# Cross-attention with image prompts: the last 64 channels' keys in two array halves, the second batch's context transposed by VectorE, the prompts projected in four 32-column tiles

## The chip, the cores and the metric

The kernel runs on one core of a Trainium2 chip. A core has five engines with a queue of instructions each: TensorE (PE, matrix products; its weight loads are listed as PEld), VectorE (DVE), ScalarE (ACT), GpSimd (POOL) and SyncE (SP, which issues most DMA transfers). Data lie in SBUF on 128 partitions; TensorE writes to PSUM banks. Engines wait for each other by semaphores, and each works through its own queue in order. The metric is the device time of one execution in microseconds (us).

TensorE is an array of 128 x 128 cells. A matmul loads weights (contraction on the array's rows, output channels on its columns) and streams a second operand through them. A matmul with fewer output channels uses a strip of the array's columns, one with a shorter contraction a strip of its rows; several strips can hold different weights.

## The reference

Eight batches, 112 queries and 375 context rows each, all float32. The first 371 context rows are text, the last 4 are image prompts. 20 heads of 16 channels, 320 channels in all.

```python
q = heads(x @ W_q); k_t = heads(text @ W_k); v_t = heads(text @ W_v)
probs_t = softmax(q @ k_t^T * scale)
text_out = probs_t @ v_t
k_ip = heads(prompts @ W_k_ip); v_ip = heads(prompts @ W_v_ip)
qsem = l2norm(probs_t @ text)                  # per head and query, 512 wide
sem = qsem @ l2norm(prompts)^T
probs_ip = softmax(q @ k_ip^T * scale + 0.5 * sem) * mask
out = (text_out + probs_ip @ v_ip) @ W_out + b_out + x
```

## The kernel before

The norm of `probs_t @ text` is never formed from the 512-wide rows. The kernel makes the inner products of all context rows with each other once a batch (`gram`, L463, and `first_gram` for batch 0), doubles what lies off the diagonal, and multiplies each head's unnormalised probabilities with these, with the values and with the prompts in one product (`product`, recorded at L710): a 112-row product per head and per block of 32 context rows. Heads are worked in five groups of four; the four heads of a group stand on four strips of 32 array rows. A step is a batch and a group, (b, g).

Per batch there are these stages, written as generators that are advanced piece by piece:

- context: loaded by SP (`load_ctx`, L135) and turned so that embedding lies on partitions (`transposed_context`, L394). Batches 0 and 1 are loaded in whole rows of 2 KB and transposed by TensorE against an identity (L414), with ScalarE and VectorE copying from PSUM (L424, L422). Batches from 2 on are loaded in pieces of 512 bytes and transposed by VectorE alone (L402). The constant `LEAD` = 2 separates them. Behind the text columns come four columns of the normalised prompts (`prompts_behind`, by GpSimd).
- values (`values`, L535): three chunks of 128 context rows, four matmuls each.
- keys (`keys`, L493): three pieces. The first two are 128 channels each, four matmuls over 371 columns. The third holds the last 64 channels, spread with zeros to 128 (each head's 16 channels take a strip of 32), since a head's scores are taken on a strip of 32 rows. For batch 0 (L512) and the last batch (`last_keys`, L526) it is a product like the others, with `wk_sb` spread by GpSimd (`spread`, L124). For batches 1 to 6 these 64 channels are computed along with the values, as 64 further output columns (L543, 384 in place of 320), copied by GpSimd into `k3` (L552) with zeros between, and transposed by TensorE (L503).
- queries (`project_queries`, L319), two batches at a time from batch 1 on: channels on partitions, multiplied by a mask that keeps the even or the odd heads of each strip of 32 (L353). For the last 64 channels only one such copy is made.
- scores (L662), maximum (VectorE, L675), exponential (ScalarE, L679), a DMA that lays the probabilities out anew (`xg`, L686, SP), a VectorE transposition (`xgT`, L698), and the products (L710).
- per group, VectorE multiplies the product with the probabilities and sums (`reduced`, L763), ScalarE takes the value sums (L737). `finish` ends a batch.
- prompts (`prompt_projections`, L275): keys and values of all 32 prompts, as two tiles of 32 array columns and 320 channels each, four matmuls a tile; then transposes and copies.

The order on TensorE, VectorE and SP is written out by hand, and after the opening that of ScalarE and GpSimd too. The opening (from L1020) runs context 0, inner products 0, values 0, queries and keys of the first two groups' heads, the scores of steps (0, 0) and (0, 1), between them the transposes of batch 1's context, then the last pieces of the keys and the first of three pieces of batch 1's inner products. From there the loop runs `alone(0)`, then pairs of steps (`pair`, L1115), and behind each pair `behind` (L1183) slips in the stages of this and the next batch. `behind(0)` holds the other two pieces of inner products, `prompt_projections`, and the first chunk of batch 1's values.

PSUM has eight banks in three rings, `qd` (4), `sc` (2) and `mm` (2). `bank` (L91) takes the next bank of a ring, from the list `turn` if that holds anything; a bank that comes round again has to be free first. The products of step (0, 0) take the four `qd` banks.

## Time and profile before

| | us |
|---|---|
| median of 3 runs | 419.94 |
| lowest and highest | 419.73, 420.93 |
| the profiled execution's own time | 421.54 |
| its span, first to last instruction | 419.8 |
| TensorE busy in the span | 411.7 (98%) |
| VectorE | 322.2 (77%) |
| ScalarE | 185.5 (44%) |
| GpSimd | 116.0 (28%) |

TensorE's granted clock is 0.999 of the full one over the span. Profile lines give an engine, a source line, what is written `<-` what is read, shapes as partitions x elements, and the count `x`. The chain is followed back from the last instruction, at each step to what released it; its pieces add up to the span. A fp32 matmul is listed as two passes, each with its weight load.

### The profile page before, as it was taken

To read this page: it belongs to the slowest core of one execution; us is meant where nothing else is said; L and a number is where in the kernel's file an instruction comes from. 1 tells how busy PE (TensorE), PEld (TensorE's weight loads), DVE (VectorE), ACT (ScalarE), POOL (GpSimd) and SP (SyncE) were. 2 spreads that over 40 slices of the span, in tenths; PEclk is the share of its full clock that TensorE was granted. 3 is DMA by queue.
4 is the path that set the end of the run, shared out by engine and by line. 5 is a ranking of instruction groups with operands and counts; after the bars stand their busy time and mean duration, and the time that the engine had idled before them with its cause. 6 is when DMAs were issued, how large, how long until landed. Compare 5 with 4: busy or idle time off the path is not lost.

```text
span 419.8 us, 13826 instructions
## 1 busy us (share of the span) xinstructions
PE 411.7 (98%) x5511; PEld 314.1 (75%) x5511; DVE 322.2 (77%) x684; ACT 185.5 (44%) x634; POOL 116.0 (28%) x278
## 2 busy tenths in 40 slices
PE   8999999999999999999999999999999999999995
PEld 8866686877677786868686877778776888776893
DVE  4054777897887876886888897887788897789964
ACT  3253333334543642514553464333643464246772
POOL 4302310031161352012051225102124126005570
PEclk9999999999999999999999999999999999999999
DMA  8678966778554656577645575575656345575311
GB/s 249 163 190 246 220 157 165 180 187 181 133 156 125 169 127 170 143 162 160 174 116 138 148 173 144 156 186 138 164 150 168 92 118 149 156 177 169 98 34 29
DMA packets 58002, 64.64 MB, mean 154 GB/s; under 512 B 19016, under 2 KB 51760, under 8 KB 57938
## 3 DMA queue, kind: packets, MB, share of 16 engines
q1 hardware_dynamic: 57054, 62.32, 58.5%
q8 instruction: 44, 0.72, 0.7%
q10 hardware_dynamic: 692, 0.89, 0.7%
q0 software_dynamic: 192, 0.55, 0.6%
q14 instruction: 20, 0.16, 0.1%
HBM read 19.04 MB, written 5.22 MB: 58 GB/s over the span
## 4 chain that ended last, share of the span: by engine, by line
PE 87%; DVE 4%; DMA 3%; ACT 2%; SPq 2%; issue 1%; ACTq 0%; POOL 0%; DVEq 0%; POOLq 0%
PE ps_qd L710 39%; PE ps_v L543 15%; PE ps_k L512 10%; PE ps_g L474 8%; PE ps_s L662 5%; PE ps_q L344 3%; PE ps_o L867 2%; DMA xg<-p 1%; DVE xgT L698 1%; PE ps_g L444 1%; DMA vr<-vd 1%; ACT p L679 1%; PE ps_c L414 1%; DVE nmx L675 1%; SPq L488 1%; DMA ct<-in_ctx_dram 1%
## 5 line engine op out<-in xcount | busy, mean ns | idle before, releaser
L710 PE MATMUL ps_qd<-u,xgT 32*112 32x40 f32 (+11 forms) x3840 | 215.7, 351 | 0.4 <-DVE xgT L698 0.4
L710 PEld LDWEIGHTS ps_qd<-u,xgT 32*112 32x112 f32 x3840 | 177.4, 172 | 38.4 <-issue 7.1
L698 DVE STREAM_TRANSPOSE xgT<-xg 128x768 f32<-128x768 f32 (+1 forms) x63 | 123.1, 1976 | 7.1 <-DMA xg<-p 7.1
L679 ACT ACTIVATE p<-ps_s,nmx 112x371 f32<-112x371 f32 x160 | 85.6, 584 | 58.3 <-DVE nmx L675 57.2
L675 DVE TENSOR_REDUCE nmx<-ps_s 112x1 f32<-112x371 f32 x160 | 77.1, 534 | 36.7 <-PE ps_s L662 34.0
L763 DVE CUSTOM_DVE_ANT_0 p<-ps_qd,p 112x371 f32<-112x371 f32 x150 | 72.7, 544 | 15.9 <-ACT pvs L737 10.4
L629 POOL COPY u<-vr 128x64 f32<-128x64 f32 x120 | 26.7, 236 | 185.0 <-PE ps_qd L710 108.0
L543 PE MATMUL ps_v<-wv_sb,ctxT 128*128 128x384 f32 (+1 forms) x192 | 63.8, 479 | 0.3 <-ACT kT L519 0.3
L662 PE MATMUL ps_s<-kT,qm 32*112 32x375 f32 (+1 forms) x320 | 60.8, 486 | 0.0
L543 PEld LDWEIGHTS ps_v<-wv_sb,ctxT 128*128 128x128 f32 x192 | 35.3, 190 | 21.2 <-ACT kT L519 1.2
L512 PE MATMUL ps_k<-ctxT,wk_sb 128*128 128x371 f32 x136 | 45.8, 481 | 0.0
L737 ACT COPY pvs<-ps_qd 112x21 f32<-112x21 f32 x150 | 21.7, 198 | 52.4 <-DVE ss L763 50.1
L512 PEld LDWEIGHTS ps_k<-ctxT,wk_sb 128*128 128x128 f32 x136 | 24.6, 190 | 13.4 <-ACT ctxT L424 0.5
L474 PE MATMUL ps_g<-ctxT 128*32 128x119 f32 (+11 forms) x672 | 33.3, 344 | 0.6 <-POOL ctxT L390 0.6
L474 PEld LDWEIGHTS ps_g<-ctxT 128*32 128x32 f32 x672 | 25.9, 109 | 8.1 <-issue 4.1
L662 PEld LDWEIGHTS ps_s<-kT,qm 32*112 32x112 f32 x320 | 27.1, 171 | 5.0 <-issue 0.5
L550 ACT COPY vext<-ps_v 128x384 f32<-128x384 f32 (+1 forms) x24 | 11.2, 465 | 37.1 <-PE ps_v L543 37.0
L681 ACT COPY ipl<-ps_s 112x4 f32<-112x4 f32 x140 | 24.0, 172 | 0.0
L353 DVE TENSOR_SCALAR qm<-ps_q,emask 128x224 f32<-128x224 f32 (+1 forms) x25 | 9.0, 398 | 18.5 <-PE ps_q L344 18.5
L460 ACT ACTIVATE ug<-ps_g 128x375 f32<-128x375 f32 (+2 forms) x24 | 9.0, 377 | 29.2 <-DMA ct<-in_ctx_dram 8.4
L519 ACT COPY kT<-ps_k 128x371 f32<-128x371 f32 x17 | 8.0, 469 | 30.5 <-PE ps_k L512 30.5
L402 DVE STREAM_TRANSPOSE ctxT<-ct 128x512 f32<-128x512 f32 x18 | 19.3, 1077 | 0.0
(157 smaller groups left out, 311.6 us busy)
## 6 DMA issues: line engine op xcount, KB each, us to landing
xg<-p SPq DMA_DIRECT2D x158, 162.3 KB
u<-ug SPq DMA_DIRECT2D x128, 99.0 KB
ct<-in_ctx_dram SPq DMA_DIRECT2D x24, 176.0 KB
vip<-vipd SPq DMA_DIRECT2D x7, 560.0 KB
vr<-vd SPq DMA_DIRECT2D x20, 120.0 KB
vd<-vext SPq DMA_DIRECT2D x14, 160.0 KB
vd<-vext SPq DMA_DIRECT2D x28, 40.0 KB
ct<-in_ctx_dram SPq DMA_DIRECT2D x4, 256.0 KB
```

Of the source, the lines that this page charges most:

```text
L474: nc.tensor.matmul(ps[p * RG : (p + 1) * RG, s0 : T - t0], ctxT[:, e, t0 + q * RG : t0 + (q + 1) * RG], ctxT[:, e, t0 + s0 : T], start=(e ...
L512: nc.tensor.matmul(ps[:, :TT], wk_sb[:, e, i * P : (i + 1) * P], s["ctxT"][:, e, :TT], start=(e == 0), stop=(e == NE - 1),)
L543: nc.tensor.matmul(ps[:, :w], ctxT[:, e, c * P : (c + 1) * P], wv_sb[:, e, :w], start=(e == 0), stop=(e == NE - 1),)
L629: nc.gpsimd.tensor_copy(region(b, c)[:, :, UV - c * P :], s["vr"][:, c * QN : (c + 1) * QN, g, :])
L662: nc.tensor.matmul(ps[:S, :w], qm[a * RG : (a + 1) * RG, i, r, j * S : (j + 1) * S], s["kT"][a * RG : (a + 1) * RG, i, :w], start=True, st ...
L675: nc.vector.tensor_reduce(nmx, ps[:S, :TT], AX.X, ALU.max, negate=True)
L679: nc.scalar.activation(p, ps[:S, :TT], AF.Exp, bias=nmx)
L681: nc.scalar.copy(s["ipl"][:, groups[g][a], :], ps[:S, TT:T])
L698: nc.vector.transpose(xT[:, j : j + n].rearrange("p j (k q) -> p q j k", q=QN), xg[:, :, j * RG : (j + n) * RG].rearrange("p q (j k) -> p ...
L710: nc.tensor.matmul(banks[a][:S, j * RG : UW], xT[a * RG : (a + 1) * RG, j, :S], region(b, c)[a * RG : (a + 1) * RG, p, q * RG :], start=(j ...
L737: nc.scalar.copy(s["pvs"][:, h, :], ps[:S, TT:UW])
L763: nc.vector.tensor_tensor_reduce(out=p, in0=ps[:S, :TT], in1=p, scale=1.0, scalar=0.0, op0=ALU.mult, op1=ALU.add, accum_out=s["ss"][:, h : ...
```

## The change

Seven edits, which belong together:

1. The last 64 channels' keys of every batch are made by `last_keys`: for each of the four embedding chunks two matmuls with the same 64 weight columns, the first half of the text rows (186) into PSUM partitions 0 to 63, the second half (185) into 64 to 127. Four ScalarE copies then lay each half into the key tile twice, on partitions 0 to 63 and 64 to 127. The values are 320 columns wide for all batches; `k3`, its copies and transposes and `spread` are gone.
2. A strip of 32 rows in the last key tile now holds two heads. Queries of the last channels get both masked copies (one more VectorE instruction in each of the five query projections), and `scores` chooses strip and copy accordingly. GpSimd copies the last 64 columns of `wq_sb` behind themselves, one instruction instead of four.
3. Batch 1's context is loaded in pieces of 512 bytes (eight transfers in place of four) and transposed by VectorE, called right behind the inner products of batch 0. Its cleared block comes first in GpSimd's queue, and the prompt copy for it stands ahead of the clearing of `xT`.
4. Batch 1's inner products are all three made in the opening, in banks `mm`, `mm`, `sc`.
5. `behind(0)` therefore begins with the prompt projections, in a `qd` bank.
6. The prompts are projected in four tiles of 32 array columns: keys and values, 160 channels each. Three ScalarE copies, one GpSimd copy, and two transfers to DRAM instead of one.
7. `prompt_logits` reads the last heads contiguously.

```diff
-    wk_sb = const.tile([P, NE, CP], F32, tag="wk_sb", name="wk_sb")
-    wv_sb = const.tile([P, NE, C + REST], F32, tag="wv_sb", name="wv_sb")
+    wk_sb = const.tile([P, NE, C], F32, tag="wk_sb", name="wk_sb")
+    wv_sb = const.tile([P, NE, C], F32, tag="wv_sb", name="wv_sb")
...
     def load_ctx(b):
-        if b >= LEAD:
+        if b > 0:
...
     def prompt_projections():
         for e in range(NE):
             for i, w in enumerate((wkip_sb, wvip_sb)):
-                nc.tensor.matmul(
-                    ps[i * N : (i + 1) * N, :C],
-                    ipT[:, e, :],
-                    w[:, e, :],
+                for n, part in enumerate(parts):
+                    m = 2 * i + n
+                    nc.tensor.matmul(
+                        ps[m * N : (m + 1) * N, : C // 2],
+                        ipT[:, e, :],
+                        w[:, e, part],
...
     def project_queries(bs):
-            for r in range(2 if i < FULL else 1):
+            for r in range(2):
...
     def transposed_context(b):
-        if b >= LEAD:
+        if b > 0:
...
     def keys(b):
-        for i in range(NC):
-            ps = bank(f"ps_k_{b}_{i}", spare=0 < b < B - 1 and i == FULL)
-            if 0 < b < B - 1 and i == FULL:
-                for c in range(NT):
-                    nc.tensor.transpose(...)
-                nc.scalar.copy(s["kT"][:, i, :TT], ps[:, :TT])
-                yield
-                return
+        for i in range(FULL):
+            ps = bank(f"ps_k_{b}_{i}")
...
+        last_keys(b, bank(f"ps_k_{b}_{FULL}", spare=0 < b < B - 1))
+        yield
     def last_keys(b, ps):
         for e in range(NE):
-            nc.tensor.matmul(
-                ps[:, :TT], wk_sb[:, e, FULL * P :], s["ctxT"][:, e, :TT], ...
-        nc.scalar.copy(s["kT"][:, FULL, :TT], ps[:, :TT])
+            for n in range(2):
+                nc.tensor.matmul(
+                    ps[n * REST : (n + 1) * REST, : min((n + 1) * KH, TT) - n * KH],
+                    wk_sb[:, e, FULL * P :],
+                    s["ctxT"][:, e, n * KH : min((n + 1) * KH, TT)],
+                    start=(e == 0),
+                    stop=(e == NE - 1),
+                )
+        for n in range(2):
+            t = slice(n * KH, min((n + 1) * KH, TT))
+            for m in range(2):
+                nc.scalar.copy(
+                    s["kT"][m * REST : (m + 1) * REST, FULL, t],
+                    ps[n * REST : (n + 1) * REST, : t.stop - t.start],
+                )
...
     def values(b):
-        w = C + REST if 0 < b < B - 1 else C
-                    ps[:, :w], ctxT[:, e, c * P : (c + 1) * P], wv_sb[:, e, :w],
+                    ps[:, :C], ctxT[:, e, c * P : (c + 1) * P], wv_sb[:, e, :],
...
     def scores(b, g, a, early=False, ps=None):
+        rg = a
+        if i == FULL:
+            rg, r = a // 2 + 2 * (a % 2), a % 2
-            qm[a * RG : (a + 1) * RG, i, r, j * S : (j + 1) * S],
-            s["kT"][a * RG : (a + 1) * RG, i, :w],
+            qm[rg * RG : (rg + 1) * RG, i, r, j * S : (j + 1) * S],
+            s["kT"][rg * RG : (rg + 1) * RG, i, :w],
...
     drain(products)
+    drain(transposed_context(1))
     gram_to_groups(0, range(QN - 1))
...
-    spread(nc.gpsimd, wq_sb)
-    nc.gpsimd.tensor_copy(wv_sb[:, :, C:], wk_sb[:, :, FULL * P : C])
-    spread(nc.gpsimd, wk_sb)
+    nc.gpsimd.tensor_copy(wq_sb[:, :, C:], wq_sb[:, :, FULL * P : C])
...
-    turn[:] = ["mm", "qd", "qd"]
-    drain(transposed_context(1))
-    prompts_behind(1)
     for a in range(GROUP):
         scores(0, 1, a, early=True)
...
-    run(("g", 1), lambda: gram(1))
+    turn[:] = ["mm", "mm", "sc"]
+    run(("g", 1), lambda: gram(1), NT)
...
     def behind(n):
-                turn[:] = ["sc", "mm", "qd", "mm"]
+                turn[:] = ["qd", "mm"]
...
             tr(0)
-            gr(nb, 2)
             if n:
+                gr(nb, 2)
                 f(b - 1)
             else:
                 run(("pp",), prompt_projections)
```

More of the change, by code (lines that the diff above doesn't have):

```diff
@@ L52 @@
     HN = H * NIP
+    KH = (TT + 1) // 2
     VW = NIP + 1 + D
@@ L245, in order_values @@
         )
+    parts = [slice(n * C // 2, (n + 1) * C // 2) for n in range(2)]
     def normalised_prompts():
@@ L310, in prompt_projections @@
         yield
-        nc.sync.dma_start(vipd, kv[N:])
+        for n, part in enumerate(parts):
+            m = 2 + n
+            nc.sync.dma_start(vipd[:, part], kv[m * N : (m + 1) * N, : C // 2])
         yield
@@ L549, in values @@
                 )
[L550 to L555 removed]
+            nc.scalar.copy(vext[:, c, :], ps[:, :C])
             yield
@@ L956, in ending @@
             )
-        parts = [slice(i * C // 2, (i + 1) * C // 2) for i in range(2)]
         ps_o = [bank(f"ps_o_{b}_0", spare=True)]
```

58 lines of the change are left out of this document (14 added, 44 removed).

## The prediction

> **What bounds the kernel now.** I read the page's busy shares and its summary of the chain first, then the chain itself in order of time, the opening 50 us instruction by instruction, the groups by shape, and the busy time in short stretches.
>
> ```profile
> PE 411.7 (98%) x5511; PEld 314.1 (75%) x5511; DVE 322.2 (77%) x684; ACT 185.5 (44%) x634; POOL 116.0 (28%) x278
> PE 87%; DVE 4%; DMA 3%; ACT 2%; SPq 2%; issue 1%; ACTq 0%; POOL 0%; DVEq 0%; POOLq 0%
> ```
>
> TensorE (PE) is busy 98% of the span and carries 87% of the chain, so what it must stream decides almost everywhere; another engine matters only where PE has to wait for it. The chain gives each PE stage its start, its length and its number of passes (one fp32 matmul is two passes, so four matmuls show as x8):
>
> ```profile
> 26.07 1.43 PE ps_c L414 x12
> 27.50 1.21 PE ps_s L662 x6
> 28.70 5.18 PE ps_k L512 x16
> 33.89 2.64 PE ps_g L474 x27
> 36.53 1.15 PE ps_qd L710 x10
> ...
> 41.88 2.19 PE ps_g L474 x43
> 44.07 2.21 PE ps_kv L280 x16
> 46.28 2.78 PE ps_v L543 x8
> 49.05 1.15 PE ps_qd L710 x10
> ...
> 59.91 2.69 PE ps_k L512 x8
> ...
> 101.51 0.32 PE ps_k L503 x3
> 101.83 2.51 PE ps_k L512 x8
> 104.34 5.16 PE ps_v L543 x16
> ...
> 138.09 0.47 PE ps_k L503 x3
> ...
> 359.44 2.17 PE ps_v L543 x8
> ```
>
> The reader should see three prices here. Eight passes over 371 columns take 2.51 us, 0.314 a pass or 0.85 ns a column. The same eight passes take 2.69 (at 59.91) when the stage before used the array in strips: a change of how the array is divided costs 0.18. And ps_kv pushes sixteen passes of 320 columns, alternating between two 32-column strips of the array, through in 2.21 us, the time that eight such passes take in one full-width array (2.17 at 359.44): two strips ran side by side almost perfectly.
>
> **The change, part by part.**
>
> *Last 64 channels, batches 1 to 6.* Gone: 64 of the 384 columns of every value chunk. A chunk goes from 2.58 (half of 5.16, at 104.34) to 2.17, so 0.41 less. There are 18 chunks; the first of batch 1 lies in the opening and is treated there, so 17 x 0.41 = 7.0 us. Gone too: three transposes a batch, 0.32 in odd batches, 0.47 in even ones (which come straight after strip work, so 0.15 of it is the change of division): 3 x 0.32 + 3 x 0.47 = 2.4 us. Added: eight matmuls a batch, 64 output channels each, over 186 or 185 columns, alternating between the two halves of the array's columns. That is sixteen passes at 186 x 0.85 = 0.157: 2.51 us if one after another, 1.26 if in pairs. No row shows 64-column strips; the nearest, ps_kv, shows pairs, so I take 1.26 and keep 2.51 as the other end. 6 x 1.26 = 7.5 us. Changes of division: in even batches the keys stand between products and inner products, one change of 0.18 to get in (the one to the inner products was there); in odd batches between queries and the next keys, two new ones: 3 x 0.18 + 3 x 0.36 = 1.6 us. Sum: -7.0 - 2.4 + 7.5 + 1.6 = **-0.3 us**. So this large-looking part is nearly a wash.
>
> *The opening* needs these rows:
>
> ```profile
> 8.15 0.29 SPq L158 DMA_DIRECT2D ct<-in_ctx_dram  x1
> 14.53 7.77 SPq L488 DMA_DIRECT2D u<-ug  x12
> 14.56 0.28 POOL L327 MEMSET xT<- 64x224 f32 x1
> 20.30 0.82 PE L344 MATMUL ps_q<-xT,wq_sb 128*128 128x112 f32 x6
> 21.16 0.58 DVE L353 TENSOR_SCALAR qm<-ps_q,emask 128x112 f32<-128x112 f32 x2 [11.40 <-PE ps_q L344]
> 25.82 1.95 ACT L679 ACTIVATE p<-ps_s,nmx 112x371 f32<-112x371 f32 x4 [0.52 <-DVE nmx L675]
> 37.03 0.50 SPq L122 DMA_DIRECT2D wip<-in_L_xattn_W_v_ip_dram  x1
> 42.11 0.54 DVE L763 CUSTOM_DVE_ANT_0 p<-ps_qd,p 112x371 f32<-112x371 f32 x1 [2.11 <-ACT pvs L737]
> 43.97 4.50 DVE L698 STREAM_TRANSPOSE xgT<-xg 128x1536 f32<-128x1536 f32 x2
> ```
> ```profile
> L698 DVE STREAM_TRANSPOSE xgT<-xg 128x1536 f32<-128x1536 f32 x17 | 51.5, 3027 | 0.0
> L402 DVE STREAM_TRANSPOSE ctxT<-ct 128x512 f32<-128x512 f32 x18 | 19.3, 1077 | 0.0
> L280 PEld LDWEIGHTS ps_kv<-wip,ipT 128*32 128x32 f32 x16 | 1.2, 110 | 0.7
> ```
> ```profile
> 13.00:14.00 1.00, 1.00 (x9) 0.92 (x8) 0.00 (x0) 0.48 (x2) 0.45 (x1) 1.00 0.23 57
> 41.00:42.00 1.00, 1.00 (x40) 0.92 (x36) 0.00 (x0) 0.10 (x2) 0.24 (x1) 1.00 0.85 322
> 44.00:45.00 1.00, 1.00 (x17) 0.55 (x9) 1.00 (x3) 0.43 (x2) 0.76 (x2) 1.00 1.01 165
> 46.00:47.00 1.00, 1.00 (x6) 0.53 (x4) 1.00 (x2) 0.42 (x1) 0.19 (x2) 1.00 1.11 285
> ```
>
> First the new wait. VectorE (DVE) now transposes the second batch's context, 3 x 1.08 = 3.2 us, early in its queue; behind it stand the query scalings, and on GpSimd (POOL) the small prompt copy waits for it, with the clearing of xT (0.28) behind, which the queries need at 20.30. DVE sat idle for 11.4 us up to 21.16, so the work itself is free if the context has landed. In the trace of before the loads run dry soon after 13 (last column: GB/s). The change brings the context in 512-byte pieces; while batch 2's came that way, from 43.5 on, traffic was 165 to 285 GB/s, while large pieces reached 322 (41 to 42). For 0.74 MB that is 2.6 to 4.5 us instead of 2.3, so it lands at 13.6 to 15.5; DVE ends at 16.8 to 18.7, and xT is clear (copy about 0.2, clearing 0.28) by 17.3 to 19.2. Covered, by 1.1 us at worst. SP's four further issues fall into its idle time between 8.4 and 14.5.
>
> Then PE, from 26.07 on. The transposes of the context (1.43) go. The second group's scores move up, but two of them need banks that the first group's second exponential frees at 25.82 + about 1.1 = 26.9; with two passes of 0.314 they end near 27.55, not 28.70 (-1.15). Keys: 2.67, then the last keys in halves 1.26 + 0.18, ending at 31.65. All inner products of batch 1 now follow here: 2.64 + 2.19 = 4.83, to 36.5. The first product started at 36.53. So nothing is won yet: all that was saved has been spent on inner products moved up, and the product ends at 41.88 as before.
>
> There the gain lies, and a new wait as well. Inner products used to cover the time in which DVE frees the products' banks. Now the prompt projection comes first and takes the first of these: free at 42.11 + 0.54 = 42.65, a PE wait of 0.8 us. Its weights, issued by 37.5, must have landed too; traffic peaks until about 42, so they come at about the same time (before, the projection at 44.07 would have hidden that). With four strips and 160 columns it takes half of 2.21, 1.1 us: 43.8. Values 2.17 + 0.2: 46.2. What is late next is DVE: its transposition for the second group starts at 43.97 and takes 3.03, so the product starts at 47.05 whatever PE does. Against 49.05: **-2.0 us**. Bounds: -2.4 if the bank wait at 26.9 does not bind; one microsecond lost for each by which the weights land after 43.6.
>
> *Hidden.* ScalarE: four copies of half the columns instead of one of all, at most the 1.95 us that four exponentials over all columns take at 25.82; after each PE has at least 2.5 us of other work before a result is wanted, and ACT is 44% busy and 2% of the chain. DVE: a second scaling of the last queries, two of 0.29 us (21.16: two in 0.58) and three over twice the columns, at most double: 2.3 us in all, on an engine that is idle for 23%. POOL loses spreads and copies; it is 0% of the chain. Taken at nothing. The last batch's keys shrink by 1.3 us, but by then the chain runs over DVE:
>
> ```profile
> 381.75 2.92 DVE xgT L698 x2
> ```
>
> so nothing there either (other end: -1.3).
>
> *Sum.* -2.0 - 0.3 = -2.3 us on the profiled execution, whose own time is 421.54 (span 419.80), 1.6 above the median of the three runs, 419.94. So 419.2 there, and 417.6 for a median.
>
> **Rivals.**
>
> *The halves do not run as a pair.* Then the keys cost 1.25 more in seven batches that count (0 to 6): +8.8, **426.4**. Against it: ps_kv. For it: that row has 32-column strips with different data, no row has 64. It decides from a pair speed-up below 1.57 on (7 x 0.34 us eats the 2.3).
>
> *Weights of one half cannot be loaded while the other half streams.* Sixteen loads at 110 ns stand bare, 1.8 us in each of seven batches: **430**. ps_kv speaks clearly against it: sixteen loads of 110 ns and sixteen passes fit into 2.21 us. The Trainium skill, "TensorE: Matmul & The Clock Gate", section "Part 3: Packing small matmuls — row/col tiling", states this rule: weight loads overlap running matmuls only when the row groups differ, and the halves share all rows. By that rule the result is the slower one above; the trace does not agree for 32-column strips.
>
> *The lead is given back.* DVE or transfers, not PE, then set the pace of batch 0's later groups. For it: DVE is the one that ends the opening at 47.05. Against it: PE carries 87% of the chain, and every row quoted between 49.05 and 138.09 is PE. All 2.0 lost: **419.6**.
>
> *The second batch's context comes late.* Each microsecond of landing after 16.6 (20.30 less 0.48 on POOL and 3.24 on DVE) holds DVE's queue, POOL's, the queries and so all of PE; it takes 18.9 to lose the gain, and about 20.2 gives **421.5**.
>
> *More.* Banks do not bind at 26.9, and the last batch's keys do count: -0.4 - 1.3, **415.9**.
>
> **How the numbers follow.** 0.3% is 1.26 us, about what a measurement of this kernel tells from no change. Forecast 0.52 (417.6, its own range 416.6 to 418.6), more 0.13, given back 0.17, no pairs 0.10, bare loads 0.02, late context 0.06. Faster, below 418.7: 0.52 + 0.13, less a little of the forecast's upper edge: 0.63. Slower, above 421.2: 0.18. Same: 0.19. The range takes in "more" and "given back" with half a microsecond or more to spare, and ends at the late context: 415.2 to 421.6, leaving out about 0.13.
>
> **What would show it.** Last keys: sixteen passes in 1.3 to 1.5 us with both halves starting within some 50 ns of each other; 2.5 proves the rival. Values of batches 1 to 6 at 2.17 a chunk. Context transposes on DVE between 14 and 19 with the queries still at 20.3; a later start shows the late context. First product still at 36.5; PE idle about 0.8 before the projection and 0.8 before the second group's product at 47.0. From there the lead over the old trace should stay near 2 us and be 2.3 at the end. I am wrong if PE shows new idle time in the batches, or if that lead shrinks before 90 us.

## The result, and the profile after

The changed kernel takes 426.02 us (median of four runs, 422.53 to 426.79); beside it the kernel before took 420.44 (419.73 to 422.69). The ratio is 1.0106, with a 95% interval of 1.0059 to 1.0154: about 1.1% slower, where I had forecast 417.6 us, 0.5% faster. Here and below, ratios leave out single executions over 1.5% above the fastest of their kernel; medians and ranges hold all of them. The profiled execution took 426.36 us, its span 424.6.

The page of the changed kernel: busy time by engine, and PE's busy tenths and granted clock in 40 slices of 10.6 us.

```profile
PE 414.2 (98%) x5609; PEld 335.7 (79%) x5609; DVE 326.4 (77%) x691; ACT 190.1 (45%) x658; POOL 112.0 (26%) x263
...
PE   8999999979999999999999999999999999999996
...
PEclk9999999997999999999999999999999999999999
```

As averages nothing has happened: PE is 98% busy in both kernels. But in PE's row there is a 7 in the ninth slice, and in the row of the clock a 7 in the tenth. Both lie between 85 and 106 us. The chain of waits of the changed kernel (start, duration, engine, tile, line) runs through that place like this:

```profile
30.40 1.40 PE ps_k L509 x15
...
36.44 1.15 PE ps_qd L695 x10
...
42.63 1.50 PE ps_kv L274 x32
...
46.99 1.22 PE ps_qd L695 x10
...
79.77 2.59 PE ps_k L492 x8
...
87.77 3.80 DMA xg<-p
91.78 1.55 DVE xgT L683
93.58 0.46 DVE nmx L660
94.06 0.57 ACT p L664
94.78 7.02 PE ps_qd L695 x46
...
104.36 1.33 PE ps_q L337 x6
...
109.78 4.31 PE ps_v L531 x16
```

Down to 82 us all is close to the forecast: the first product at 36.4, the second at 46.99 (forecast 47.05, before 49.05), the keys in halves in 1.40 us. At 79.77 PE is 2.5 us ahead of the kernel before (keys of batch 1 at 79.77 here, at 82.25 there). Then the chain leaves PE for 7 us: a transfer of xg, VectorE's (DVE's) transposition of it, the maxima of the next scores behind that and an exponential, and only then a product. At 104.36 PE is 4.2 us behind (100.18 before). So 6.7 us are lost between 82 and 104, and nothing like that happens later.

PE's timeline in that place (the bracket is the idle time ahead of the row), and PE and its clock in windows of 5 us (first figures: length and PE's busy time; the third figure from the end is the granted clock):

```profile
87.55 1.22 PE L695 MATMUL ps_qd<-u,xgT 32*112 32x392 f32 x10 [0.55 <-POOL u L612]
...
94.78 7.02 PE L695 MATMUL ps_qd<-u,xgT 32*112 32x392 f32 x55 [1.95 <-ACT ipl L666]
```

```profile
85.00:90.00 5.00, 4.45 (x92) 4.15 (x87) 1.70 (x1) 1.13 (x3) 2.74 (x8) 1.00 0.69 171
90.00:95.00 5.00, 3.05 (x63) 2.90 (x56) 3.17 (x7) 0.94 (x3) 0.50 (x3) 0.98 1.09 250
95.00:100.00 5.00, 5.00 (x44) 4.88 (x46) 3.87 (x10) 1.96 (x10) 0.24 (x1) 0.50 0.59 166
100.00:105.00 5.00, 5.00 (x85) 4.95 (x80) 1.99 (x4) 1.98 (x7) 0.84 (x4) 0.83 0.37 88
```

The loss has two halves. PE rests for 0.55 + 1.95 = 2.5 us. Behind the rest it works at a granted clock of 0.50 and then 0.83, and that costs, as an estimate from the two windows, 5 x 0.50 + 5 x 0.17 = 3.35 us more. Together 5.85 of the 6.7. (The first, short rest is for GpSimd's copy of values into u; what it copies was sent by SP's vr transfers, issued from 82.65 us on, 79.51 before.)

Who was late? DVE's timeline, of the changed kernel and then of the kernel before: the transposition for step (1,1). (The maxima of the scores of step (1,2), 93.58 in the chain, stand behind it.)

```profile
91.78 1.55 DVE L683 STREAM_TRANSPOSE xgT<-xg 128x768 f32<-128x768 f32 x1 [5.08 <-DMA ct<-in_ctx_dram]
```

```profile
88.97 1.58 DVE L698 STREAM_TRANSPOSE xgT<-xg 128x768 f32<-128x768 f32 x1 [0.64 <-DMA xg<-p]
```

DVE sat idle for 5.08 us, for the xg that landed at 91.6 (the row names a transfer of ct; the chain above names xg, from 87.77 to 91.57). Before, it had waited for the same xg for 0.64 us only. The transfer goes back to SP's queue; its timeline, of the changed kernel and of the one before:

```profile
51.52 5.91 SPq L671 DMA_DIRECT2D xg<-p  x4
57.53 3.38 SPq L480 DMA_DIRECT2D u<-ug  x4
...
69.77 1.06 SPq L305 DMA_DIRECT2D vipd<-kv  x2
70.87 3.79 SPq L556 DMA_DIRECT2D vd<-vext  x6
74.70 0.43 SPq L1217 DMA_DIRECT2D x_sb<-in_x_dram  x1
75.23 4.84 SPq L671 DMA_DIRECT2D xg<-p  x4
...
84.92 4.00 SPq L671 DMA_DIRECT2D xg<-p  x4
```

```profile
51.74 4.01 SPq L686 DMA_DIRECT2D xg<-p  x4
55.86 2.50 SPq L488 DMA_DIRECT2D u<-ug  x4
...
67.93 0.59 SPq L312 DMA_DIRECT2D vipd<-kv  x1
68.56 2.75 SPq L573 DMA_DIRECT2D vd<-vext  x6
71.36 0.44 SPq L1236 DMA_DIRECT2D x_sb<-in_x_dram  x1
72.41 4.52 SPq L686 DMA_DIRECT2D xg<-p  x4
...
82.65 3.66 SPq L686 DMA_DIRECT2D xg<-p  x4
```

Where no line is left out, each row begins where the one above it ends: in the changed kernel SP issues without a pause of more than 0.1 us from 56.6 to 92 us, and the issue itself is the work, 0.4 to 0.9 us for most transfers. So a delay is never made up. Four groups of issues are longer than before: xg at 51.5 (+1.9: the fourth of them waited 2.4 us for a piece of the third batch's context to land), u (+0.9), vipd (two issues, +0.5) and vd (+1.0). The kernel before still had two pauses to lose (0.7 us at 58.4, and 0.6 ahead of the xg at 72.41), so the sum of 4.3 becomes less: SP is 2.8 us late at the xg of step (1,0) and 2.3 at those of (1,1). PE is 2.5 us early at the same time. Between them they have used up the slack.

Of the four delays only vipd's 0.5 us is the edit's own. u's and vd's are one slow issue each (1.48 us against 0.59, 1.45 against 0.42). The wait for the context is 2.4 us here; in the trace of pool_issue (below), whose edits all lie behind it, it is 0.2 at the xg and 0.9 at the u behind them. So these three come and go between executions, and why they met in this one is not shown. Once they had met, SP had no pause left in which to make them up.

### The profile page after: what moved, and what is told of

Read it like the earlier page. It is cut to its first block, busy times and chain, and to the rows that moved or that the text cites. A ratio compares the mean times of both kernels' runs of the same rounds, so it can differ in the third digit from the quotient of the medians.

```text
span 424.6 us, 14043 instructions
## 1 busy us (share of the span) xinstructions
PE 414.2 (98%) x5609; PEld 335.7 (79%) x5609; DVE 326.4 (77%) x691; ACT 190.1 (45%) x658; POOL 112.0 (26%) x263
## 4 chain that ended last, share of the span: by engine, by line
PE 88%; DVE 6%; DMA 2%; ACT 2%; issue 1%; ACTq 0%; POOL 0%; DVEq 0%; SPq 0%; POOLq 0%
PE ps_qd L695 40%; PE ps_v L531 13%; PE ps_k L492 9%; PE ps_g L466 8%; PE ps_s L647 6%; PE ps_q L337 3%; DVE xgT L683 2%; DMA xg<-p 2%; PE ps_k L509 2%; PE ps_o L852 2%; PE ps_g L436 1%; DVE nmx L660 1%; DVE p L748 1%; PE ps_w L423 1%; ACT p L664 1%
## 5 line engine op out<-in xcount | busy, mean ns | idle before, releaser
L695 PE MATMUL ps_qd<-u,xgT 32*112 32x40 f32 (+11 forms) x3840 | 223.4, 356 | 3.8 <-ACT ipl L666 2.0
L695 PEld LDWEIGHTS ps_qd<-u,xgT 32*112 32x112 f32 x3840 | 194.5, 174 | 30.4 <-issue 8.8
L647 PE MATMUL ps_s<-kT,qm 32*112 32x375 f32 (+1 forms) x320 | 64.1, 486 | 0.0
L531 PE MATMUL ps_v<-wv_sb,ctxT 128*128 128x320 f32 x192 | 56.1, 439 | 0.3 <-ACT kT L499 0.3
L492 PE MATMUL ps_k<-ctxT,wk_sb 128*128 128x371 f32 x128 | 43.6, 484 | 0.0
L647 PEld LDWEIGHTS ps_s<-kT,qm 32*112 32x112 f32 x320 | 31.7, 173 | 3.9 <-ACT p L664 0.4
L492 PEld LDWEIGHTS ps_k<-ctxT,wk_sb 128*128 128x128 f32 x128 | 23.0, 190 | 13.2 <-issue 1.3
L394 DVE STREAM_TRANSPOSE ctxT<-ct 128x512 f32<-128x512 f32 x21 | 22.2, 1069 | 5.9 <-DMA ct<-in_ctx_dram 5.9
L538 ACT COPY vext<-ps_v 128x320 f32<-128x320 f32 x24 | 10.2, 425 | 30.1 <-PE ps_v L531 30.0
L453 POOL TENSOR_TENSOR ug<-ug,half 128x128 f32<-128x128 f32 (+1 forms) x24 | 10.6, 447 | 27.7 <-ACT ug L452 27.7
```

The lines of the kernel that those rows point to most:

```text
L394: nc.vector.transpose(ctxT[:, :, c * P : (c + 1) * P].rearrange("p e (j i) -> p j e i", i=RG), ct[:, some, :].rearrange("p j (k e) -> p j ...
L492: nc.tensor.matmul(ps[:, :TT], wk_sb[:, e, i * P : (i + 1) * P], s["ctxT"][:, e, :TT], start=(e == 0), stop=(e == NE - 1),)
L531: nc.tensor.matmul(ps[:, :C], ctxT[:, e, c * P : (c + 1) * P], wv_sb[:, e, :], start=(e == 0), stop=(e == NE - 1),)
L647: nc.tensor.matmul(ps[:S, :w], qm[rg * RG : (rg + 1) * RG, i, r, j * S : (j + 1) * S], s["kT"][rg * RG : (rg + 1) * RG, i, :w], start=True ...
L695: nc.tensor.matmul(banks[a][:S, j * RG : UW], xT[a * RG : (a + 1) * RG, j, :S], region(b, c)[a * RG : (a + 1) * RG, p, q * RG :], start=(j ...
```

## The experiments

The theory to be tested ("SP's queue"): SP, not PE, sets the pace from 50 to 92 us; SP became late; PE rests for it, and the low clock doubles the price. The rivals: the keys in halves cost more in every batch than the values give ("keys"); the clock falls by itself ("clock"); too many bytes are in flight ("bytes"). All times, with the kernel before beside each (times in us, runs in brackets, the ratio with its 95% interval):

| run | time | before | ratio |
|---|---|---|---|
| queue_light | 424.88 (421.55 to 426.62) | 421.12 | 1.0082 (1.0051 to 1.0114) |
| before_light | 420.94 (420.10 to 422.96) | 421.12 | 1.0010 (0.9989 to 1.0031) |
| keys_only | 426.24 (422.89 to 426.54) | 421.12 | 1.0103 (1.0055 to 1.0151) |
| filled | 424.24 (423.68 to 426.73) | 421.12 | 1.0082 (1.0051 to 1.0113) |
| wip_first | 426.89 (422.10 to 427.81) | 420.56 | 1.0138 (1.0090 to 1.0185) |
| light2 | 420.53 (419.91 to 426.05) | 420.56 | 1.0016 (0.9975 to 1.0057) |
| light2_wip | 420.61 (419.82 to 423.23) | 420.56 | 0.9989 (0.9965 to 1.0012) |
| before_light2_wip | 425.66 (424.40 to 427.54) | 420.56 | 1.0102 (1.0052 to 1.0151) |
| pool_issue | 420.60 (419.49 to 421.16) | 420.96 | 1.0002 (0.9984 to 1.0020) |
| loads_moved | 422.37 (419.75 to 425.90) | 420.96 | 1.0046 (1.0018 to 1.0074) |
| paired | 418.88 (417.82 to 424.40) | 420.96 | 0.9952 (0.9927 to 0.9978) |
| best | 419.89 (417.41 to 424.08) | 420.96 | 0.9984 (0.9955 to 1.0012) |
| before_late | 425.71 (424.45 to 427.31) | 421.01 | 1.0122 (1.0086 to 1.0158) |
| paired_only | 421.93 (420.65 to 425.82) | 421.01 | 1.0036 (1.0003 to 1.0069) |
| pool_paired | 420.32 (417.34 to 424.24) | 421.01 | 0.9974 (0.9941 to 1.0007) |
| pool_paired_wip | 419.91 (418.62 to 420.40) | 421.01 | 0.9975 (0.9958 to 0.9992) |

**queue_light.** The first try at making SP's queue lighter, with ScalarE (ACT) as the other issuer:

```diff
-            nc.sync.dma_start(vipd[:, part], kv[m * N : (m + 1) * N, : C // 2])
+            nc.scalar.dma_start(vipd[:, part], kv[m * N : (m + 1) * N, : C // 2])
...
-            values_to_dram(nb, nc.sync)
-            if b == 0:
+            values_to_dram(nb, nc.scalar if b == 0 else nc.sync)
+            if b == 2:
                 nc.sync.dma_start(x_sb[:, 5:, :], x[5:].rearrange("b s c -> s b c"))
```

> The changed kernel with nine transfers taken off SP's queue in front of batch 1: the six vd<-vext of batch 1 (3.79 us on SP) and the two vipd<-kv (1.06 us) are issued by ScalarE, and x_sb for batches 5 to 7 (0.43 us) is loaded one batch and a half later. Theory 'queue' (SP's queue runs late from 56 us on, the last xg of step (1,1) lands at 91.6 us instead of 88.9, VectorE turns it late, the scores' banks come free late, PE waits 2.5 us in 87 to 95 and the granted clock then falls to 0.50 for 5 us, which costs 3.35 us more): the xg of step (1,1) land by 87 us, the wait at 92.8 and the low clock are gone, time 419.0 to 421.0. Rival 'keys' (what was lost is lost in the batches, by the halves): within 1 us of the changed kernel, 425 to 427. Rival 'clock' (the clock falls by itself, whatever PE waits for): 423 to 424.5, with the clock still low after 90 us.

Measured 424.88, with executions from 421.55 to 426.62. The profiled one took 422.12; the rest at 93 us and the low clock behind it are gone, as "SP's queue" says, but another rest of 1.24 us stands at 72.43, because ACT now issues when it should compute exponentials. The theory's 419.0 to 421.0 is missed: the fastest of the ten runs took 421.55, and the profiled one is the second fastest, so what the slower ones lost is not shown. ACT was the wrong engine to give the work to; GpSimd (POOL), idle from 60 to 70 us, came later (pool_issue).

**before_light.** The kernel before with the same edits (one vipd in place of two).

> The kernel before, with the same transfers taken off SP's queue (here one vipd). Theory 'queue': nothing in 80 to 100 us waited for SP in the kernel before but 0.64 us of VectorE, so the time stays within 0.7 us of before, 419.7 to 421.1. Rival (SP's queue set the pace before, too): 417 to 419.

420.94 against 421.12: no difference. SP's queue is nearly full in the kernel before, too, but nothing of weight waits for it.

**keys_only.** The opening as before, the keys and the prompts' tiles as changed:

```diff
-    drain(transposed_context(1))
     gram_to_groups(0, range(QN - 1))
...
+    turn[:] = ["mm", "qd", "qd"]
+    drain(transposed_context(1))
+    prompts_behind(1)
...
-    run(("g", 1), lambda: gram(1), NT)
+    run(("g", 1), lambda: gram(1))
...
-            if n:
-                gr(nb, 2)
+            gr(nb, 2)
```

> The changed kernel with its opening as before: batch 1's context transposed by PE, its inner products two pieces before the first groups and two behind. What is left of the change is the last 64 channels' keys in halves, the narrower values and the prompts' four 32-column tiles. The prediction's terms for it: -0.3 us, 419.5 to 421. Rival 'keys' (the halves cost more in the batches than the values give): 422 to 425. If the two vipd and the later transfers alone bring the wait at 93 us, it shows here, too, with a low clock behind it: 422 to 426.

426.24, as slow as the whole change. Its trace has rests of 2.33 us at ps_kv (for the second load of wip, which landed at 45.7), 1.11 and 0.99 us at 90 and 96, and no low clock behind them: the way to the loss is in part another one. So the edits of the opening aren't needed for a loss of this size; transfers that come late are enough, and how much of it the two vipd make is not shown. Why wip came late in this kernel is not settled; it also did so in single executions of others.

**filled.** Six products of the identity where PE waits, into columns that nobody reads:

```diff
+        if one == (1, 0):
+            for i in range(6):
+                nc.tensor.matmul(st[b]["qd", g][i % GROUP][:S, UW:],
+                                 ident[:, :S], ident[:, : 512 - UW],
+                                 start=False, stop=False)
         products_in(*two, (tags[1],) * 2 + (tags[0],) * 2)
```

> The changed kernel with six products of the identity (about 0.3 us each, 2 us in all, into 120 columns that nobody reads) put where PE waits 1.95 us at 92.83 us. Theory 'queue' with 'a PE at rest lowers the granted clock': PE's next product starts as late as in the changed kernel (94.8 us) but the clock stays near 1.00 in 95 to 105 us, and the time is 2.5 to 3.5 us under the changed kernel's, 422.5 to 423.5. Rival 'clock' (it falls whatever PE does): unchanged, 425.5 to 427, the clock 0.5 to 0.8 in 95 to 105 us.

424.24; inconclusive. In the profiled execution wip landed late (44.65), PE rested 0.84 and 1.21 us at ps_kv, and the granted clock was 0.93 and 0.72 in the two 5 us windows from 40 us on. After so late an opening there was no rest left at 93 us to be filled.

**wip_first.** wip is issued ahead of the four xg of step (0,1):

```diff
+    load_embed(nc.sync, wkip_sb, w_k_ip)
+    load_embed(nc.sync, wvip_sb, w_v_ip)
     for a in range(GROUP):
         scores(0, 1, a, early=True)
         probabilities(0, 1, a)
-    load_embed(nc.sync, wkip_sb, w_k_ip)
-    load_embed(nc.sync, wvip_sb, w_v_ip)
```

> The changed kernel with the two loads of the prompts' weights (wip) issued on SP ahead of the four xg of step (0,1), not behind them. What is known by now: in the changed kernel, and in the runs queue_light, keys_only and filled, PE rests 3.8, 2.9, 4.4 and 2.1 us that it does not rest in the kernel before, at ps_kv (0.8 to 2.3 us, for wip, which landed at 41.9 to 44.6 us), at product (0,1) and at the products of batch 0's end; span less rest less the low clock is 417 to 419 in all of them. Theory 'transfers' (PE's lead makes the transfers the pace in 37 to 95 us; what PE waits for is whichever lands last): wip lands about 38 to 40 us, ps_kv waits for nothing (-0.8 to -2.3 us there), but the xg of (0,1) land 4 us later, and PE rests 1 us or more at product (0,1) or behind 85 us: 423 to 426. Rival 'one late load' (wip alone is at fault): no rest after 45 us, 418.5 to 420.5.

426.89, no gain. The trace is of the fastest of its five executions (422.10), so where the others lost 3 to 5 us more is not shown. In it wip has landed by 40.6, and PE still waits 0.83 us at ps_kv: that wait is for the bank, as the prediction had it. Product (0,1) now waits 1.22 us and product (1,1) 0.88, and the clock stays at 1.00. One late load was not the cause.

**light2.** POOL issues the six vd of batch 1 and the two vipd; wo, bias and the mask are loaded 20 us later, x_sb in a smaller first part:

```diff
-            nc.sync.dma_start(vipd[:, part], ...)
+            nc.gpsimd.dma_start(vipd[:, part], ...)
...
-                nc.sync.dma_start(x_sb[:, 1:5, :], x[1:5].rearrange("b s c -> s b c"))
+                nc.sync.dma_start(x_sb[:, 1:3, :], x[1:3].rearrange("b s c -> s b c"))
...
-            values_to_dram(nb, nc.sync)
+            values_to_dram(nb, nc.gpsimd if b == 0 else nc.sync)
             if b == 0:
-                nc.sync.dma_start(x_sb[:, 5:, :], x[5:].rearrange("b s c -> s b c"))
+                load_channels(nc.gpsimd, wo_sb, w_out)
+                nc.gpsimd.dma_start(sm_sb, smask.unsqueeze(1))
+                nc.gpsimd.dma_start(bias_sb, b_out.partition_broadcast(S))
```

> The changed kernel with less in the queues in 43 to 90 us: vd<-vext of batch 1 and vipd are issued by GpSimd in place of SP, wo, bias and smask (0.54 MB) are loaded 20 us later, and of x_sb only batches 1 and 2 are loaded at 43 us (0.29 MB in place of 0.57; the others behind step (1,3)). Theory 'transfers': what is left is the wait for wip at ps_kv (0.8 to 2.3 us) and 0.5 us at product (0,1); none behind 55 us, so no low clock behind it; 419.5 to 422. Rival 'keys' (lost in the batches): 425 to 427, with PE's rest gone and the time still there.

420.53: 5.5 us less than the changed kernel, though two of its ten runs still took over 425. In the trace (of the fastest run) PE rests 0.83 and 0.45 us in the opening and nowhere between 50 and 300 us; the clock is 1.00 throughout. "Keys", as an account of the 5.6 us lost, is dead.

**light2_wip and before_light2_wip.** light2 with wip first, and the same on the kernel before.

> Both: the lighter queues and wip ahead of the xg of (0,1). Theory 'transfers': no rest of PE over 0.6 us before 300 us, clock 1.00 throughout, 418 to 420, which is under the kernel before by 1 to 2.5 us. Rival 'keys': 423 to 426.

> The kernel before, with the same two moves of transfers. Theory 'transfers': it had no rest to lose there, so 419.5 to 421.5, within 0.3% of before. Rival (any kernel gains by lighter queues): 417 to 419.

light2_wip takes 420.61, the same as light2, where the theory had 418 to 420: a rest of 1.51 us has moved to product (0,1). The control on the kernel before was the surprise, 425.66, which neither theory expected. Its trace shows a rest of 2.62 us at 74.41: the chain there is POOL, which issues vipd, vd, wo, the mask and bias one after the other from 70.6 to 76.7, then makes the copy that PE's next product waits for. The windows, with the clock:

```profile
75.00:80.00 5.00, 2.97 (x32) 2.78 (x36) 1.31 (x6) 0.30 (x2) 2.38 (x7) 0.71 0.97 235
80.00:85.00 5.00, 5.00 (x97) 4.79 (x91) 2.82 (x9) 2.02 (x8) 0.00 (x0) 0.95 1.01 187
```

One rest of 2.6 us, put into the kernel before by accident, makes it as slow as the changed one: from 0.3 us ahead of the kernel before at 67 us it is 4.3 behind at 80. The rest and the clock behind it explain the size of the loss without the change.

**pool_issue and loads_moved** take light2 apart: the issues alone (vd and vipd on POOL), and the bytes alone (wo, bias, mask loaded in the opening, x_sb split).

> The changed kernel with the six vd<-vext of batch 1 and the two vipd<-kv issued by GpSimd, nothing else moved; it tells SP's places in the queue from the bytes in flight. Theory 'SP's queue': SP is 4.9 us less busy ahead of the xg of step (1,0), which lands in time, and the time is that of light2, 420 to 421.5. Theory 'bytes' (too much is in flight in 40 to 57 us, which makes the fourth xg of (0,3) wait 2.4 us): the xg of (0,3) are as late as in the changed kernel, but SP has caught up by 75 us, so it is 420 to 422 here, too, unless PE rests before 75 us; only with such a rest 423 to 426.

> The changed kernel with fewer bytes in 43 to 57 us and SP's queue as it was: wo, bias and smask (0.54 MB) are loaded by GpSimd 25 us earlier, of x_sb only batches 1 and 2 are loaded at 43 us, the others behind step (1,3). Theory 'SP's queue': SP still has the two vipd and six vd in front of the xg of batch 1, PE rests 1 to 2 us behind 85 us and the clock falls: 423 to 426. Theory 'bytes': no xg waits at 54 us, SP runs 1.5 to 2.4 us earlier all the way to 89 us, as early as in the kernel before, and the rest at 93 us shrinks from 1.95 us to under 0.7: 420 to 422.

pool_issue gives 420.60, all of light2's gain, with no load moved; its runs lie within 1.7 us. loads_moved gives 422.37, with runs up to 425.90: 3.65 of the 5.4 us. It lies between the two expectations. In its trace no xg waits over 0.5 us for the context, SP has a pause of 1.1 us ahead of the xg at 59.96, and PE doesn't rest behind 50 us; what it loses is a rest of 1.95 us for wip at ps_kv and the low clock behind that. So the bytes are one way in which SP becomes late, and to shorten its queue is enough. SP's timeline of pool_issue:

```profile
66.62 0.59 SPq L1217 DMA_DIRECT2D x_sb<-in_x_dram  x1
69.88 4.09 SPq L671 DMA_DIRECT2D xg<-p  x4
...
80.13 3.65 SPq L671 DMA_DIRECT2D xg<-p  x4
```

SP now pauses from 67.2 to 69.9, for the probabilities: it waits for PE's side again and not the other way round. The xg of step (1,1) go out at 80.13, not 84.92. The Trainium skill, "DMA: Bandwidth & Descriptors", section "Rules for kernel authors", says that spreading transfers over several issuing engines does not give more bandwidth, that "it only saves sequencer issue time". The runs agree, and here the issue time was what was short: worth 5.4 us between the two medians.

**before_late** is the converse: the kernel before, with eight small loads that nobody reads on SP's queue, and nothing else.

```diff
                 nc.sync.dma_start(x_sb[:, 5:, :], x[5:].rearrange("b s c -> s b c"))
+                for i in range(8):
+                    nc.sync.dma_start(extra[:, i, :], x[i, :, :8])
```

> The kernel before, with eight small loads that nobody reads (112 rows of 32 B each) put on SP's queue behind the load of x_sb at 71.8 us, ahead of the xg of step (1,0): SP alone is made late, by about 0.45 us each, 3.6 us in all. Theory 'SP's queue': the xg of (1,0) and (1,1) go out 3.6 us later, which is more than VectorE's 0.64 us of idle time behind them, PE rests 1 to 3 us in 85 to 97 us, the granted clock falls to 0.5 to 0.8 for 5 us behind it, and the kernel before becomes as slow as the changed one: 423 to 427. Rival (lateness of SP is hidden and something else of the change is at fault): 420 to 421.5.

425.71: SP's lateness alone makes the kernel before as slow as the changed one. The xg of step (1,1) go out at 87.59, 4.9 us later than before, while PE is 1.5 us late; in the changed kernel SP was 2.3 us late and PE 2.5 early, so SP falls behind PE by 3.4 us here and by 4.8 there. PE's timeline, and the windows:

```profile
97.79 1.58 PE L711 MATMUL ps_qd<-u,xgT 32*112 32x392 f32 x13 [1.77 <-ACT ipl L682]
```

```profile
95.00:100.00 5.00, 3.23 (x60) 2.54 (x56) 4.96 (x9) 2.19 (x8) 0.24 (x1) 0.98 0.87 218
100.00:105.00 5.00, 5.00 (x61) 3.99 (x59) 2.21 (x10) 0.71 (x4) 0.47 (x2) 0.67 0.70 159
```

The same row waits for the same thing (a bank that ACT's ipl copy frees), followed by the same fall of the clock, to 0.67. (This execution was 1.2 us late in the opening already; between 67 and 104 us it loses 4.4 against before_light.)

The rival "clock" has nothing for it: in the 18 traces the granted clock falls five times between 20 and 410 us, each time within or behind a rest of 1.2 us or more (the changed kernel, filled, loads_moved, before_late, before_light2_wip).

**paired** is about what was left. light2 no longer loses anything at 93 us, but it is not 2.3 us faster than before either. Its stretches of products and scores take longer where the scores of a batch's last group stand in them. PE's timeline, from a stretch's first product to the keys behind it, in light2, in the kernel before, and in paired:

```profile
341.16 1.22 PE L695 MATMUL ps_qd<-u,xgT 32*112 32x392 f32 x10
...
349.30 0.60 PE L647 MATMUL ps_s<-kT,qm 32*112 32x375 f32 x2
...
349.61 0.47 PE L647 MATMUL ps_s<-kT,qm 32*112 32x375 f32 x1
...
349.74 0.47 PE L647 MATMUL ps_s<-kT,qm 32*112 32x375 f32 x1
...
352.41 1.83 PE L492 MATMUL ps_k<-ctxT,wk_sb 128*128 128x371 f32 x5
```

```profile
342.29 1.22 PE L710 MATMUL ps_qd<-u,xgT 32*112 32x392 f32 x10
...
353.05 1.20 PE L512 MATMUL ps_k<-ctxT,wk_sb 128*128 128x371 f32 x3
```

```profile
340.50 1.22 PE L695 MATMUL ps_qd<-u,xgT 32*112 32x392 f32 x10
...
348.95 0.48 PE L647 MATMUL ps_s<-kT,qm 32*112 32x375 f32 x2
...
351.26 2.76 PE L492 MATMUL ps_k<-ctxT,wk_sb 128*128 128x371 f32 x8
```

11.25 us in light2, 10.76 before, for the same 208 matmuls. In light2 the scores no longer start two at a time. The change had put heads 2 and 3 on the second and fourth row group of the array and heads 0 and 1 on the first and third; paired takes them in another order, so that the third and fourth go together, then the first and second, as in all other groups:

```diff
+    def together(g, heads):
+        if g // 2 < FULL:
+            return heads
+        return {LOW: (0, 2), HIGH: (1, 3)}[heads]
...
-        for a in heads:
+        for a in together(steps[n][1], heads):
```

> light2 with another order of the scores of each batch's last group: heads 1 and 3 together (third and fourth row group of the array), then 0 and 2 (first and second), where light2 and the changed kernel have 2 and 3 (second and fourth), then 0 and 1 (first and third). In light2 the stretches of products that such scores stand in are 0.09 to 0.55 us longer than in the kernel before, 2.36 us in batches 1 to 6, and in the last batch 1.64 us longer, 0.86 us of it rest. Theory 'rows out of step' (two scores on row groups that products do not meet side by side leave one row group behind, and PE takes up its work in order): these stretches take what they took before, -2.4 us and up to -0.8 in the last batch: 417 to 418.5, under the kernel before by 0.5 to 0.9%. Rival (the stretches are longer for another reason, as the shared last keys' four copies): as light2, 420 to 421.

The stretch is back at 10.76, and the time is 418.88, a little over the expected 417 to 418.5: 0.5% under the kernel before, the first that beats both kernels beyond the uncertainty. The last batch's long stretch, 23.65 us in light2, is not shorter (23.75). That the order is the cause of the long stretches is shown; why (PE takes up its work in order, so one row group that is behind holds the others) is argued, though the single starts above speak for it.

**best, pool_paired, pool_paired_wip, paired_only.** best adds to paired a bank for ps_kv from the other pool (turn `["mm", "mm"]`), the xg of step (0,1) turned in two halves, and loads_moved in place of light2's late wo. The others put the pairs on pool_issue, on pool_issue with wip first and the two halves, and on the changed kernel with nothing else.

> All that helped, and two more edits in the opening: the scores paired as in 'paired', vd and vipd of batch 1 on GpSimd, wo, bias and smask loaded in the opening, x_sb split, the projected prompts in a bank of the pool of keys and values (they waited 0.83 us for a product's bank), and xg of step (0,1) turned in two halves, so that its product can start behind the first. -2.4 to -3.2 from the pairs, -0.5 to -1.3 from the opening against light2: 415.5 to 418. If the transfers set the pace again, PE rests once more behind 70 us and it is 419 to 422.

> The changed kernel with the pairs of scores as in 'paired' and its queues as they were. If the two causes are separate, the batches are 2 us shorter (stretches of products at 10.70 to 10.76 us in place of 10.79 to 11.25), while the rest at 93 us and the low clock stay: 423 to 424.5. If the rest came from the scores out of step: 418 to 420.

> The changed kernel with the two cures that measured best alone: vd and vipd of batch 1 issued by GpSimd (420.6) and the pairs of scores (-1.7 to -2 us against light2). Nothing else is moved. Theory: 418.3 to 419, ratio 0.993 to 0.997. In runs in which wip lands late PE rests 1 to 2 us at ps_kv: 420 to 421 there.

> pool_paired, with wip ahead of the xg of step (0,1) and that step's xg turned in two halves. Theory 'whichever transfer is last': no rest at ps_kv but for the bank (0.83 us), up to 1 us at product (0,1) in its place; if the halves hide it, 417.5 to 418.5 and fewer runs over 420; if not, as pool_paired.

best reached 417.41 in one run, but its median, 419.89, misses the expected 415.5 to 418 and is no better than paired's: in the profiled execution PE rested 1.07 us at ps_kv, for wip. paired_only gave 421.93, 4.1 us less than the changed kernel, where separate causes were to give 423 to 424.5. In its profiled execution, the fastest of ten, the stretches are short, and the two rests are still there (0.96 and 0.65 us, at 87 and 93), so the causes look separate; but after these shorter rests the clock stayed at 1.00. Why the rests are shorter is open: PE had also rested 0.79 us for wip in the opening, which leaves it less of a lead. pool_paired, 420.32 where 418.3 to 419 was expected, runs from 417.34 to 424.24, and its median is only 0.3 us under pool_issue's; its trace has a rest of 2.09 us for wip. With wip first and that step's xg turned in two halves (pool_paired_wip, 419.91) no run is over 420.40 and none under 418.62: the two edits together cost about 1 us in the good runs and take away the bad ones.

## Why the prediction was wrong, step by step

**The keys, the values, the opening: right.** Sixteen half passes take 1.40 us behind the queries (forecast 1.26 and 0.18), so two 64-column halves do run side by side; the two rivals on that point fall. That also contradicts, here, the rule that the prediction weighed from the Trainium skill, "TensorE: Matmul & The Clock Gate", section "Part 3: Packing small matmuls — row/col tiling" (weight loads overlap running matmuls only when the row groups differ): the two halves share all rows. That the first rival's price, 426.4, lies within 0.4 us of the measured time is chance; its mechanism is not there. The values of a pair of chunks went from 5.16 to 4.31, 0.43 a chunk (0.41). The first product came at 36.4 (36.5), the bank wait at ps_kv was 0.83 (0.8), the projection took 1.5 (1.1) without harm, since VectorE's transposition ended only at 46.84, and the second product started at 46.99 (47.05). At 80 us the lead was 2.5.

**The second batch's context: covered, with nothing to spare.** VectorE's timeline of the changed kernel:

```profile
16.68 3.07 DVE L394 STREAM_TRANSPOSE ctxT<-ct 128x512 f32<-128x512 f32 x3 [5.94 <-DMA ct<-in_ctx_dram]
```

The queries still started at 20.24. But the context landed some 1.1 us later than the latest time of the forecast (13.6 to 15.5), just at the 16.6 from which each microsecond was to be lost. That this rival cost nothing was luck. (By its own rule, landing at 20.2 gives 421.2, not 421.5.)

**"Hidden": the step that failed.** It lists ScalarE, VectorE and GpSimd and takes them at nothing; SP's queue is missing from it, and so is what a lead of PE does to the slack behind that queue. The runs showed SP 2.3 us late and PE 2.5 early at the xg of step (1,1), a rest of PE of 2.5 us and some 3.35 us of low clock behind it. I counted the second vipd nowhere (0.5 us of the 2.3). The rival "the lead is given back" names "DVE or transfers", and I argued it down because every quoted row of the chain between 49 and 138 us is PE. But a chain shows who ended last, not by how much: the transposition for step (1,1) had followed its xg by 0.64 us of waiting even before, and SP had only two pauses, 0.7 and 0.6 us. A lead of PE is worth nothing there unless SP gets earlier too, and SP got later. The rival had the mechanism; its price (all of 2.0 lost) was off by 6.4 us, since I had no term for SP's own delay nor for the clock. So "that lead shrinks before 90 us", named as what would prove me wrong, is what happened.

**A term that was not in the sum: the scores' rows.** With the transfers out of the way (light2) the lead goes from 2.56 us at 80 to 0.64 behind the last batch's queries (373.67 in the trace of before, 373.03 in light2's). From the starts in PE's timeline, behind 78 us: 15 value chunks -6.40, keys of batches 1 to 6 +6.34, stretches of products +2.36 where the forecast had nothing, queries +0.28, a rest of 0.58 at 183 us that only the kernel before had: sum +2.0, against 1.92 seen. I had read the new row groups in the scores' code and given them no price. paired brings the products of the batches down by 2.0 of these 2.4 us.

**The last batch: right in sum by luck.** The last keys save 1.29 us (I had 0 and, at the other end, 1.3), but the last batch's products take 1.64 longer, 0.86 of it rest.

**The base.** The sum stood against a span of 419.80 us that ends 4.56 us behind DVE's last row (414.64 + 0.60 us). In the changed kernel, light2 and before_light that distance is 3.1 to 3.3. The profiled execution of before was 1.3 us longer at its end than usual; so even light2's span of 418.2 is no gain, and its ratio (1.0016) says the same.

All in all: -2.1 in the opening as forecast; +1.8 from there to the end where -0.3 was forecast (light2's lead is 0.3 us at DVE's last row), hence about nothing for the change without its queue trouble (pool_issue: 1.0002); and, by the medians, some 5.5 us from SP's queue, PE's rest and the clock behind it.

## What to carry to other kernels

Before a gain on the bounding engine is counted, take each queue that feeds it through the next 50 us: how long are its issues, has it pauses left, and by how much did the data come before it was wanted? An engine that is 98% busy can have 0.6 us of slack on its inputs, and a lead of 2 us will then be met by a wait. And where parts of an array are worked on in a fixed order, a new order of row groups is an edit with a price, even if not one matmul is added.

## What the runs showed of the hardware that I had not expected

A rest of PE of about 2 us can cost 1.7 to 2.7 times its length. Behind rests of 1.77 us (before_late), 1.95 (the changed kernel, and again loads_moved) and 2.62 (before_light2_wip), the granted clock of the 5 us window behind or around its end was 0.67, 0.50, 0.66 and 0.71. In windows cut at the edges each fall is one to 0.50: for 6.8 us in the changed kernel (94.85 to 101.66) and for 3.4 us in before_late (99.86 to 103.25, 2.1 us behind the rest's end), before_light2_wip and loads_moved. By these lengths the falls cost an estimated 3.4 and 1.7 us each. It is not a fixed threshold: behind 2.09 (pool_paired) and 2.33 us (keys_only) the next windows show 1.00. The Trainium skill, "TensorE: Matmul & The Clock Gate", section "HAM oscillation — how this bites in real kernels", warns of idle gaps over about 3.4 us. That the clock goes to half agrees with the 0.50; the length doesn't, shorter rests were enough here. The Trainium skill says on the same page, in section "Part 1: The HAM clock gate (the "warmup" mystery)", that the window it is judged by runs freely; that would fit rests of the same length with and without a fall, but no run here shows the window.

Executions of one kernel differ by up to 5.9 us (pool_paired: 417.34 to 423.19 in eleven of twelve), and by 1.8 with wip issued earlier and that xg turned in halves (pool_paired_wip). With the same order of issues in the opening, the last part of wip landed at 42.8 us in the traces of the changed kernel and light2, at 44.65 in that of filled and at 45.2 in that of pool_paired; why is left open.
